# Encoder stages one slot later, their statistics split over two slots, and the last output sum on VectorE

## The chip, the cores and the metric

The kernel runs on one core of a Trainium2 chip. A core has five engines with queues of their own: TensorE (PE: matmuls and transposes, with weight loads shown as PEld), VectorE (DVE), ScalarE (ACT), GpSimd (POOL) and SyncE (SP, which issues the DMAs here). PE writes into PSUM, of which the kernel uses eight banks of 128 x 512 fp32. The metric is the device time of one execution in microseconds.

## The reference

One encoder layer over a context of 77 tokens, and one decoder layer over 2048 tokens, for 2 batches, width 512, 16 heads of 32, feed-forward width 2048, all in fp32 and with norms ahead of each part:

```python
x = x + _mha(_ln(x, enc_n1_s, enc_n1_b), _ln(x, ...), enc_in_w, ..., enc_out_w, ..., eb)   # src: 77 tokens
h = _ln(x, enc_n2_s, enc_n2_b)
memory = x + (jax.nn.relu(h @ enc_ff1_w.T + enc_ff1_b) @ enc_ff2_w.T + enc_ff2_b)
yn = _ln(y, dec_n1_s, dec_n1_b)                                                            # tgt: 2048 tokens
y = y + _mha(yn, yn, dec_sa_in_w, ..., sb)              # causal, with a relative bias
y = y + _mha(_ln(y, dec_n2_s, dec_n2_b), memory, dec_ca_in_w, ..., cb)
h = _ln(y, dec_n3_s, dec_n3_b)
y = y + (jax.nn.relu(h @ dec_ff1_w.T + dec_ff1_b) @ dec_ff2_w.T + dec_ff2_b)
```

`_mha` projects to q, k and v, takes softmax(q k / sqrt(32) + bias) v by heads, and projects out.

## The kernel before

The order of all work is written out by hand, each engine executing its instructions in the order of the program, and waits between engines by semaphores.

The first part is the decoder's causal self-attention. Its 2048 tokens of a batch are four blocks of 512. A *unit* is one tile of 128 query tokens (t) of one group of four heads (g) in one block (b, m): 16 units a block, 128 in all. For a unit, PE computes the scores of the four heads in pieces of up to four key tiles, one bank for each head (line L374); VectorE reads the banks into `pp` and takes the maximum, by L383 for the far keys and L390 for the last two tiles, where the bias is added; ScalarE takes the exp (L404); PE transposes the probabilities (`turn`, L424); ScalarE and VectorE copy the transposes to `pts` (L430, L428); PE multiplies them with v (`values`, L452). Scores run two units ahead of values. The banks come from a ring (`bank()` gives the one that was taken longest ago; `values` takes one out while its sum is held).

Between a unit's turn and the next scores, a *slot* runs side work: first the list `light[n]`, then the projections `jobs[n]` of coming blocks (q_job L215, part_job L1038, out_job L251), then the list `late[n]`. A list `behind[n]` runs after scores of a later unit and before the values. The slots hold, among others, the norm of coming blocks (`norm_load`, `norm_stats`, `norm_center`, `norm_turn`, the last with a bank for each token tile that ScalarE, L310, or VectorE, L312, empties) and the whole encoder.

The encoder is a generator of 28 stages, numbered from 0 here. Both batches' 77 tokens stand in `e`, a stretch of `pp` that the small units of the first two blocks leave free; its weights of 1 MB each are loaded into stretches of `vv` that are still free, two stages ahead of use.

| stage | work |
|---|---|
| 0 to 9 | first norm, q, k, v, scores and softmax |
| 10 | turn_p(0): transposes of batch 0's probabilities (L632), copied by VectorE (L633) |
| 11 | times_v(0) (L640), turn_p(1) |
| 12 | rows_of batch 0 (output projection, L593; sum by VectorE, L596), times_v(1) |
| 13 | rows_of batch 1; load of a bias row |
| 14 | `stats`: for each batch bn_stats (L557), bn_aggr, an add (L560) on VectorE and a power on POOL (L561) |
| 15 | centring on VectorE (L567), add of the bias row on POOL (L651) |
| 16 | turned: transposes (L573), scale and shift to `nTa` by VectorE (L579) |
| 17 to 20 | first(i): L585, relu on VectorE (L647), and the load of a later weight |
| 21 | turned again, without scale (copies L577) |
| 22 to 25 | second(i): L756, sums on VectorE (L759), a load |
| 26, 27 | the cross-attention's keys and values (L585, L593), stored to DRAM (L773, L774) |

Before, stages 0 to 9 are in `late[0]` to `late[9]`, 10 to 12 in `late[11]` to `late[13]`, 13 in `light[14]`, 14 in `behind[15]`, and 15 to 27 in `late[16]` to `late[28]`. Slots 0 to 15 belong to the block m = 0, 16 to 31 to m = 1; unit 32 begins m = 2, whose probabilities need the stretch of `pp` in which the encoder works.

The second part of the kernel runs the feed-forward of all eight blocks with cross-attention beside it. The products are of the Strassen-Winograd kind: seven block products and sums instead of eight products. `second_product` finishes each with four sums on VectorE (L1554 to L1561) into `mixed` and one 128 x 512 sum on POOL into `ys` (L1564); `store` then issues the output DMAs (L1570). The last block's last product ends the kernel.

Of the kernel before, what the change touches and what calls it, by code (L numbers as in the profile page):

```python
# [12 lines left out]
ALU = mybir.AluOpType  # L13
# [5 lines left out]
B, T, S, D = 2, 2048, 77, 512  # L19
# [35 lines left out]
def tile_encoder_decoder(ctx: ExitStack, tc: tile.TileContext, ins, out):  # L55
    nc = tc.nc
    x, src = ins["x"], ins["ctx_1024"]
# [3 lines left out]
    def wchunk(name, c0, n=D):  # L61

        return ins[name][:, c0 : c0 + n].rearrange("(c p) o -> p c o", p=P)
# [18 lines left out]
    def row_into(t, name):  # L82
        i = _ROWS.index(name)
        nc.sync.dma_start(t, ins["rows"][i : i + 1, :].to_broadcast([P, D]))
# [74 lines left out]
    with (  # L159
# [20 lines left out]
        def bank():  # L180

            ring.append(ring.pop(0))
            return psum[:, ring[-1], :]
# [168 lines left out]
        def exps(k):  # L352

            for _ in range(min(k, len(late_exps))):
                late_exps.pop(0)[1]()
# [152 lines left out]
        def encoder():  # L508
# [28 lines left out]
            def weight(i, view):  # L537

                w = vv[:, 4 * i : 4 * i + 4, :]
                nc.sync.dma_start(w, view)  # L540
                return w

            def load_row(name):
                i = _ROWS.index(name)
                nc.sync.dma_start(row, ins["rows"][i : i + 1, :].to_broadcast([S, D]))
# [4 lines left out]
            ws = {}  # L550
            keep = {}

            def stats():
                for b in range(B):
                    st = sm.tile([P, 6], F32, name="bnst", tag="bnst")
                    mv = sm.tile([P, 2], F32, name="emv", tag="emv", bufs=2)
                    nc.vector.bn_stats(st[:S], e[:, b, :])  # L557
                    nc.vector.bn_aggr(mv[:S], st[:S])
                    rs = sm.tile([P, 2], F32, name="ers", tag="ers", bufs=2)
                    nc.vector.tensor_scalar_add(rs[:S, 0:1], mv[:S, 1:2], EPS)  # L560
                    nc.gpsimd.tensor_tensor(rs[:S, 1:2], rs[:S, 0:1], mhalf[:S, 0:1], ALU.pow)  # L561
                    keep["norm", b] = mv, rs
# [27 lines left out]
            def rows_of(xT, f0, b, w, add, dst):  # L590
                mm = bank()
                for c in range(NC):
                    nc.tensor.matmul(  # L593
                        mm[:S, :], xT[:, f0 + c, ts(b, S)], w[:, c, :], start=(c == 0), stop=(c == NC - 1)
                    )
                nc.vector.tensor_tensor(dst, mm[:S, :], add, ALU.add)  # L596
# [59 lines left out]
            def stage():  # L656
                stats()
                ws["q"] = weight(1, wchunk("enc_in_wT", 0))
                ws["k"] = weight(2, wchunk("enc_in_wT", D))
                ws["v"] = weight(3, wchunk("enc_in_wT", 2 * D))  # L660
                load_row("enc_bv")
# [56 lines left out]
            yield stage  # L718

            def stage():  # L720
                rows_of(oTa, 0, 1, ws["o"], e[:, 1, :], e[:, 1, :])
                load_row("enc_ff2_b")

            yield stage
            yield stats

            def stage():
                for b in range(B):
# [224 lines left out]
        gp, ve = nc.gpsimd, nc.vector  # L953
# [126 lines left out]
        blocks = [(b, m) for b in range(B) for m in range(NMB)]  # L1080
        NU = NC * TB
        jobs = {n: [] for n in range(-1, len(units) + NU)}
        light = {n: [] for n in range(-1, len(units) + NU)}
        late, behind = {n: [] for n in light}, {n: [] for n in light}

        for x, (b, m) in enumerate(blocks):
            u = x * NU
# [27 lines left out]
            for t in range(TB):  # L1115
                end = x == len(blocks) - 1
# [68 lines left out]
                norm_turn(0, 0, t - 2, apart=True)  # L1185
                warm(6)
        for n, stage in enumerate(encoder()):
            if n == 13:
                light[n + 1].append(stage)
            elif stage.__name__ == "stats":  # L1190
                behind[n + (n >= 10)].append(stage)
            else:
                late[n + (n >= 10)].append(stage)
        light[-1].append(lambda: row_into(bo, "dec_sa_out_b"))
        light[0].append(lambda: [self_bias(relg, vg, g) for g in range(1, NC)])
        light[1].append(lambda: make_bias(0, rel, v))
# [38 lines left out]
        def y_of(x, t):  # L1235
            return ys[x % 3][:, t, :]
# [113 lines left out]
        for n, k in enumerate((0, 2, 4, 10)):  # L1350
# [17 lines left out]
        TWO = (  # L1368
            ("11", "11", 0, True, "11"),
            ("S1", "T1", 1, True, "22"),  # L1370
            ("S2", "T2", 0, False, "12"),
            ("S4", "22", 1, False, "12"),
            ("S3", "T3", 0, False, "22"),
            ("12", "21", 1, True, "11"),
            ("22", "T4", 0, False, "21"),
        )
# [53 lines left out]
        def next_w(c):  # L1430
            used[0] += 1
            assert used[0] <= fed[0]
            return w_ring[(used[0] - 1) % len(w_ring)].rearrange("p (c o) -> p c o", c=c)
# [14 lines left out]
        mixed = oflat[:, H * S : H * S + 12 * P].rearrange("p (k n) -> p k n", n=P)  # L1448
# [51 lines left out]
        def start_turn():  # L1500
            p = turn_of[0] % 2
            turn_of[0] += 1
            return pairs[p], pairs[1 - p]
# [32 lines left out]
        def second_product(x, j, part):  # L1536
            if j == 0 and part == 0:
                chains[0] = start_turn()
            name, by, chain, fresh, to = TWO[j]
            i1, i2 = chains[0][chain]  # L1540
            for k in range(2 * part, min(2 * part + 2, 7)):
                bank_i, col = ((i1, 0), (i1, 1), (i1, 2), (i2, 1), (i2, 2), (i2, 0), (i2, 3))[k]
                lhs, w = lefts[j][k], next_w(4)
                for c in range(4):
                    nc.tensor.matmul(  # L1545
                        psum[:, bank_i, ts(col, P)], lhs[:, c, :], w[:, c, :],
                        start=fresh and k in (0, 3) and c == 0, stop=c == 3, skip_group_check=True,
                    )
            one = psum[:, i1, :].rearrange("p (k n) -> p k n", n=P)
            two = psum[:, i2, :].rearrange("p (k n) -> p k n", n=P)  # L1550
            c0 = 4 * (j % 2)
            if part == 1:
                nc.scalar.copy(mixed[:, 11], one[:, 0])
                ve.tensor_tensor(  # L1554
                    mixed[:, c0 : 9 : 8 - c0], one[:, 1:3], mixed[:, 11:12].to_broadcast([P, 2, P]), ALU.add
                )
            if part < 3:
                return
            ve.tensor_tensor(mixed[:, 9:11], two[:, 1:3], mixed[:, 8:9].to_broadcast([P, 2, P]), ALU.add)
            ve.tensor_tensor(mixed[:, c0 + 1 : c0 + 4 : 2], two[:, 0:2], mixed[:, 9:11], ALU.add)  # L1560
            ve.tensor_tensor(mixed[:, c0 + 2], two[:, 3], mixed[:, 10], ALU.add)  # L1561
            r, c = int(to[0]) - 1, int(to[1]) - 1
            dst = ys[x % 3][:, 2 * r : 2 * r + 2, ts(c, TOK)]
            gp.tensor_tensor(dst, dst, mixed[:, c0 : c0 + 4].rearrange("p (t o) n -> p t (o n)", t=2), ALU.add)  # L1564
            done = [t for t in ((0, 1) if j == 5 else (2, 3) if j == 6 else ())]
            b, m = blocks[x]

            def store():
                for t in done:
                    nc.sync.dma_start(out_rows[b, m, :, t, :], y_of(x, t))  # L1570

            if x == len(blocks) - 1:
                store()
            elif done:
                after[x * per + FIRST + 4 * j + 3 + 3] = store
# [152 lines left out]
        end = len(units)  # L1728
# [13 lines left out]
        def score_next():  # L1742
            n, k0, kn = stream[at[0]]
            scores(n, k0, kn)
            scored_to[n] = k0 + kn
            at[0] += 1
# [5 lines left out]
        while i < len(stream):  # L1752
            n = stream[i][0]
            pair = [p for p in stream[i : i + 2] if p[0] == n]
            while scored_to.get(n) != size[n]:
                score_next()
            while any(u == n for u, _ in late_exps):
                exps(1)
            ends = pair[-1][1] + pair[-1][2] == size[n]
            turn(pair)  # L1760
            if n == end - 2:
                for _, k0, _ in pair:
                    feed(k0 + 4)
            turned_to[n] = pair[-1][1] + pair[-1][2]
            if ends and n + 1 < end:
                slot(n + 1)
            exps((0, 2, 1, 1)[units[n][1]])
            for _ in range(2 if len(pair) > 1 and units[n][1] else 1):
                if may_score():
                    score_next()  # L1770
            if ends:
                for f in behind[n + 1]:
                    f()
            values(pair)
            while may_score() and (len(pair) > 1 or units[n][1] == 0):
                score_next()
            i += len(pair)
# [68 lines left out]
```

## Time and profile before

| | us |
|---|---|
| median of 3 runs | 2768.12 (2767.57 to 2771.48) |
| profiled execution, whole time | 2771.65 |
| its span, first to last instruction | 2769.9 |
| PE busy | 2724.6 |
| DVE, ACT, POOL busy | 1807.0, 1538.8, 915.6 |
| mean granted PE clock | 0.995 of full speed |

The span is 1.75 us shorter than the profiled execution's time, and that is 3.5 us over the median. A row of the timeline gives start and length in us, engine, line, operation, output and inputs, and the count of merged instructions; in brackets stands the idle time ahead of it and the instruction that ended that. A row of the windows gives busy us (and instructions) of PE, PEld, DVE, ACT and POOL, then the granted PE clock, the DMA share and GB/s.

### The profile page before, as it was taken

The numbers are of one execution on the slowest core, as the hardware profiler recorded it, in microseconds if no ns is written. First come the engines' busy times: TensorE is split into PE (matmuls) and PEld (weight loads), VectorE is DVE, ScalarE is ACT, GpSimd is POOL, SyncE is SP. The second block draws the span as 40 slices with busy tenths as digits, with TensorE's granted clock in tenths as the row PEclk, the third lists the DMA queues.
The fourth block names the chain that finished last, engine by engine and source line by source line (L and its number), as shares of the span: only waits on it lengthen the run. The fifth ranks groups of instructions, "written<-read, shape, count | busy, mean of one in ns | idle before, by whom it ended". The sixth has DMA issues, their size and how long they took to land.

```text
span 2769.9 us, 67113 instructions
## 1 busy us (share of the span) xinstructions
PE 2724.6 (98%) x26294; PEld 2154.4 (78%) x26294; DVE 1807.0 (65%) x5312; ACT 1538.8 (56%) x2993; POOL 915.6 (33%) x777
## 2 busy tenths in 40 slices
PE   9999999999999999999999999999999999999998
PEld 5577776677776567676677777898989898989898
DVE  5775587787776587677687783556464646464645
ACT  3444567667777557677667786444444444444431
POOL 1501135300100413213200003364646464646456
PEclk9999999999999999999999999999999999999999
DMA  8433345311112422233211004565657564656465
GB/s 225 141 97 113 106 124 178 118 55 48 47 40 70 130 78 68 72 100 115 95 50 35 29 29 158 184 227 160 225 160 239 170 223 162 222 162 222 148 225 183
DMA packets 282254, 362.47 MB, mean 131 GB/s; under 512 B 39072, under 2 KB 156624, under 8 KB 281810
## 3 DMA queue, kind: packets, MB, share of 16 engines
q1 hardware_dynamic: 281938, 358.18, 41.4%
q8 instruction: 208, 3.41, 0.5%
q14 instruction: 108, 0.88, 0.1%
HBM read 314.49 MB, written 43.59 MB: 129 GB/s over the span
## 4 chain that ended last, share of the span: by engine, by line
PE 89%; DVE 4%; ACT 3%; issue 1%; POOL 1%; DMA 1%; SPq 0%; POOLq 0%; DVEq 0%; ACTq 0%
PE psum L424 17%; PE psum L1516 14%; PE psum L1545 12%; PE psum L374 9%; PE psum L452 8%; PE psum L1038 4%; PE psum L251 4%; PE psum L215 4%; PE psum L1676 3%; PE psum L1633 3%; ACT pp L404 3%; DVE pp L383 2%; PE psum L860 2%; PE psum L830 1%; PE psum L868 1%
## 5 line engine op out<-in xcount | busy, mean ns | idle before, releaser
L404 ACT ACTIVATE pp<-pp,nm 128x128 f32<-128x128 f32 (+15 forms) x512 | 611.8, 1201 | 34.5 <-DVE nm L399 34.0
L383 DVE TENSOR_SCALAR_CACHE_REDUCE pp<-psum 128x512 f32<-128x512 f32 (+3 forms) x1024 | 555.5, 591 | 75.0 <-PE psum L374 73.4
L424 PE MATMUL psum<-ident,pp 128*128 128x128 f32 x4352 | 536.4, 278 | 20.2 <-ACT pp L404 13.5
L430 ACT COPY pts<-psum 128x512 f32<-128x512 f32 (+2 forms) x736 | 386.5, 580 | 298.9 <-PE psum L424 258.0
L424 PEld LDWEIGHTS psum<-ident,pp 128*128 128x128 f32 x4352 | 478.5, 142 | 79.4 <-issue 24.9
L374 PE MATMUL psum<-kT,q 32*128 32x512 f32 (+3 forms) x2560 | 321.6, 559 | 4.6 <-ACT nT L310 2.6
L452 PEld LDWEIGHTS psum<-pts,vv 128*32 128x32 f32 x8704 | 226.7, 110 | 122.5 <-DVE pp L383 67.5
L428 DVE COPY pts<-psum 128x512 f32<-128x512 f32 (+3 forms) x400 | 249.5, 654 | 106.6 <-PE psum L424 104.4
L1545 PE MATMUL psum<-pp 128*128 128x128 f32 x2560 | 304.5, 276 | 1.9 <-POOL pp L956 1.6
L1545 PEld LDWEIGHTS psum<-pp 128*128 128x128 f32 x2560 | 296.3, 192 | 8.6 <-issue 2.8
L452 PE MATMUL psum<-pts,vv 128*32 128x128 f32 x8704 | 279.5, 276 | 6.7 <-DVE pp L383 4.2
L956 POOL TENSOR_TENSOR pp<-pp 128x512 f32<-128x512 f32 x159 | 212.6, 1354 | 126.5 <-DMA pp<-in_dec_ff_wT_dram 66.5
L1516 PE MATMUL psum<-vv,pp 128*128 128x256 f32 x1024 | 236.2, 381 | 0.0
L374 PEld LDWEIGHTS psum<-kT,q 32*128 32x128 f32 x2560 | 138.4, 183 | 125.6 <-issue 53.6
L1516 PEld LDWEIGHTS psum<-vv,pp 128*128 128x128 f32 x1024 | 190.3, 190 | 25.8 <-issue 0.5
L390 DVE CUSTOM_DVE_ANT_0 pp<-psum,bias 128x256 f32<-128x256 f32 (+1 forms) x512 | 196.2, 411 | 13.8 <-PE psum L374 13.6
L1529 DVE TENSOR_TENSOR kT<-kT,psum 128x512 f32<-128x512 f32 x96 | 65.8, 686 | 191.1 <-PE psum L1516 190.9
L1516 PE MATMUL psum<-nT,pp 128*128 128x256 f32 x768 | 174.1, 380 | 0.0
L1532 ACT ACTIVATE kT<-kT,vecs 128x256 f32<-128x256 f32 x192 | 87.0, 501 | 156.6 <-DVE kT L1529 155.9
L489 POOL TENSOR_TENSOR oT<-rirows,oT 128x512 f32<-128x512 f32 x30 | 38.4, 1280 | 377.9 <-DMA rirows<-rec 269.8
L1516 PEld LDWEIGHTS psum<-nT,pp 128*128 128x128 f32 x768 | 144.2, 190 | 20.3 <-issue 1.6
L266 POOL TENSOR_TENSOR xr<-xr,row_dec_sa_out_b 128x512 f32<-128x512 f32 x30 | 38.2, 1274 | 352.9 <-DMA xr<-in_x_dram 304.9
(243 smaller groups left out, 3907.5 us busy)
## 6 DMA issues: line engine op xcount, KB each, us to landing
pp<-w_d SPq DMA_DIRECT2D x520, 256.0 KB
pp<-in_dec_ff_wT_dram SPq DMA_DIRECT2D x112, 256.0 KB
wqk<-in_dec_sa_in_wT_dram SPq DMA_DIRECT2D x76, 256.0 KB
bias<-tzg SPq DMA_DIRECT2D x128, 128.0 KB
pp<-wo_d SPq DMA_DIRECT2D x56, 256.0 KB
vv<-in_enc_ff_wT_dram SPq DMA_DIRECT2D x8, 1024.0 KB
xr<-in_x_dram SPq DMA_DIRECT2D x32, 256.0 KB
vv<-y SPq DMA_DIRECT2D x32, 256.0 KB
```

Source lines behind the costliest of these rows:

```text
L215: nc.tensor.matmul(mm, w[:, c, :], nTs[b, m][:, c, :], start=(c == 0), stop=(c == NC - 1))
L374: nc.tensor.matmul(banks[r][:, : kn * P], q[rows4(r), ts(t, P)], kT[rows4(r), g, k0 * P : (k0 + kn) * P], start=True, stop=True,)
L383: nc.vector.tensor_scalar(p[:, k0 : k0 + far], s[:, :far], 1.0, None, ALU.mult, ALU.max, accum_out=st["mx"][:, r, c : c + 1],)
L390: nc.vector.tensor_tensor_reduce(p[:, k0 + far : i + 1], s[:, far:kn], near[:, 2 - (kn - far) :], 1.0, LOWEST, ALU.add, ALU.max, accum_out ...
L404: nc.scalar.activation(p, p, AF.Exp, bias=nm, accum_out=to)
L424: nc.tensor.transpose(pt[:, ts(x, P)], state[n]["p"][r][:, k], ident)
L428: nc.vector.tensor_copy(pts[:, : len(load), :], pt[:, :w])
L430: nc.scalar.copy(pts[:, : len(load), :], pt[:, :w])
L452: nc.tensor.matmul(ot[rows4(r)], vv[:, k, ts(g * HC + r, HD)], got.pop((n, k, r)), start=k == k0 and (whole or not begun), stop=k == k1 - ...
L956: engine.tensor_tensor(out, a, b, ALU.subtract)
L1516: nc.tensor.matmul(mm[:, ts(f, TOK)], a[:, c, ts(f, P)], b[:, c, :], start=fresh and f == 0 and c == 0, stop=c == 1, skip_group_check=True,)
L1545: nc.tensor.matmul(psum[:, bank_i, ts(col, P)], lhs[:, c, :], w[:, c, :], start=fresh and k in (0, 3) and c == 0, stop=c == 3, skip_group_ ...
```

## The change

The stages 10 to 12 go from `late[11]`–`late[13]` to `late[12]`–`late[14]`. Stage 13 goes from `light[14]` to `light[15]` and begins with the statistics of batch 0; stage 14, now the statistics of batch 1 alone, goes from `behind[15]` to `light[16]`, ahead of that slot's projections. The stages 15 to 27 go from `late[16]`–`late[28]` to `late[17]`–`late[29]`. The list `behind` is gone. In `second_product` the sum into `ys` of the last block's last product runs on VectorE; all others stay on POOL.

```diff
-            def stats():
-                for b in range(B):
+            def stats(batches=range(B)):
+                for b in batches:
...
             def stage():
+                stats([0])
                 rows_of(oTa, 0, 1, ws["o"], e[:, 1, :], e[:, 1, :])
                 load_row("enc_ff2_b")
 
             yield stage
-            yield stats
+            yield lambda: stats([1])
...
-        late, behind = {n: [] for n in light}, {n: [] for n in light}
+        late = {n: [] for n in light}
...
         for n, stage in enumerate(encoder()):
-            if n == 13:
-                light[n + 1].append(stage)
-            elif stage.__name__ == "stats":
-                behind[n + (n >= 10)].append(stage)
+            if n in (13, 14):
+                light[n + 2].append(stage)
             else:
-                late[n + (n >= 10)].append(stage)
+                late[n + 2 * (n >= 10)].append(stage)
...
-            gp.tensor_tensor(dst, dst, mixed[:, c0 : c0 + 4].rearrange("p (t o) n -> p t (o n)", t=2), ALU.add)
+            end = x == len(blocks) - 1 and j == len(TWO) - 1
+            (ve if end else gp).tensor_tensor(
+                dst, dst, mixed[:, c0 : c0 + 4].rearrange("p (t o) n -> p t (o n)", t=2), ALU.add
+            )
...
-            if ends:
-                for f in behind[n + 1]:
-                    f()
             values(pair)
```

## The prediction

> **What bounds the kernel now.** I read the page first, then the waits of TensorE (PE) between 96 and 350 us, which is where the moved encoder stages lie, then the timeline of those slots, and last the last fifteen microseconds.
>
> ```profile
> span 2769.9 us, 67113 instructions
> PE 2724.6 (98%) x26294; PEld 2154.4 (78%) x26294; DVE 1807.0 (65%) x5312; ACT 1538.8 (56%) x2993; POOL 915.6 (33%) x777
> PE 89%; DVE 4%; ACT 3%; issue 1%; POOL 1%; DMA 1%; SPq 0%; POOLq 0%; DVEq 0%; ACTq 0%
> ...
> PE psum L424 <- DVE mx L390: 2.7, 2, 2.0
> PE psum L374 <- ACT nT L310: 2.1, 1, 2.1
> PE psum L424 <- ACT nT L310: 1.4, 1, 1.4
> ```
>
> PE is busy for 98% and makes 89% of the chain, so a change that only reorders work can win no more than the idle time of PE, 2769.9 - 2724.6 = 45 us in the whole span, and the time in which PE runs slowly. The change touches slots 11 to 29 and the tail. In the wait rows (total, times, longest) two stalls lie inside the moved stretch: 2.1 us before scores L374, and 2.0 of the 2.7 us before transposes L424. The 1.4 us stall comes before slot 11 ends; nothing ahead of it moves, so it stays.
>
> **Part 1: slot 11, the bank of a transposed norm.** Columns: start, length, engine, line, operation, count.
>
> ```profile
> 110.01 1.27 PE L632 MATMUL psum<-ident,pp 77*77 77x77 f32 x16
> 111.20 0.48 PE L374 MATMUL psum<-kT,q 32*128 32x128 f32 x2
> ...
> 112.26 1.48 ACT L310 ACTIVATE nT<-psum,vecs 128x128 f32<-128x128 f32 x4
> ...
> 113.79 0.81 PE L374 MATMUL psum<-kT,q 32*128 32x128 f32 x6 [2.10 <-ACT nT L310]
> ...
> 114.53 1.51 PE L452 MATMUL psum<-pts,vv 128*32 128x128 f32 x24
> ...
> 115.97 3.68 PE L424 MATMUL psum<-ident,pp 128*128 128x128 f32 x16
> ```
>
> Eight banks go round in a ring; one is held by the sums, seven are left. Slot 11 takes two for the norm's tokens 2 and 3, then turn_p(0) (L632) takes four, then the four heads' scores: the second head meets the bank of token 2, which ScalarE empties only at 112.26 + 1.48 = 113.74, behind the exps. With turn_p(0) one slot later the scores take the four banks before it and run at once. So do the values (L452 x24); of the transposes the first load gets a free bank and the second meets token 2's bank. PE then does two short things in place of L632: 8 scores (about 0.5) and 24 value products. The same shapes elsewhere give the price:
>
> ```profile
> 51.46 0.86 PE L452 MATMUL psum<-pts,vv 128*32 128x128 f32 x24
> 52.25 1.97 PE L424 MATMUL psum<-ident,pp 128*128 128x128 f32 x16
> ```
>
> 110.1 + 0.5 + 0.86 + a quarter of 1.97 gives idle from about 111.95 instead of 111.7, still until 113.79: **0.3 us** less. ScalarE sets that end and isn't changed. That is little; the second half of the price is the clock. The x24 above took 1.51 instead of 0.86 and the x16 3.68 instead of 1.97. The windows' view says why (length, PE, PEld, DVE, ACT, POOL, granted clock):
>
> ```profile
> 106.22:109.64 3.42, 2.02 (x17) 1.78 (x18) 3.38 (x19) 2.78 (x9) 0.86 (x1) 1.00 0.00 0
> 109.64:113.05 3.41, 2.05 (x23) 1.78 (x21) 3.15 (x10) 3.41 (x11) 0.00 (x0) 1.00 0.03 7
> 113.05:116.46 3.41, 2.67 (x33) 1.99 (x34) 1.15 (x10) 0.69 (x2) 3.26 (x3) 0.50 0.01 2
> 116.46:119.88 3.42, 3.42 (x16) 3.31 (x16) 0.89 (x2) 1.64 (x5) 1.74 (x2) 0.50 0.00 0
> ...
> 157.42:160.84 3.42, 2.61 (x14) 2.40 (x15) 3.19 (x14) 1.43 (x3) 0.54 (x1) 1.00 0.02 5
> ...
> 1133.65:1137.06 3.41, 3.16 (x28) 1.11 (x28) 3.41 (x15) 3.41 (x7) 2.01 (x2) 1.00 0.00 0
> 1137.06:1140.47 3.41, 3.41 (x46) 3.03 (x37) 1.69 (x11) 1.20 (x4) 3.33 (x4) 0.50 0.00 0
> ```
>
> I laid the windows on one grid of 3.41 us, and every half-clock spell of this trace fills whole cells of it: two cells, 6.8 us, behind this stall. A cell with 2.02 us of PE work keeps the clock and one with 2.05 loses it, and so does one with 3.16, which is nearly all 32-row scores (L374). So it is not busy time alone; narrow work seems to count little (my reading, from three rows). The cell 109.64 to 113.05 held 77-row transposes and two 32-row scores; after the change it holds 0.9 us of full-row value products and a first load of 128-row transposes, and idles 1.1 instead of 1.4 us. I expect it to keep the clock. Price of the spell: (1.51 - 0.86) + (3.68 - 1.97) + half of the 0.81 of the six scores, about **2.8 us**; bounds 0 (the spell stays) and 2.8.
>
> The row gives half clock behind a cell that was 60% busy. [...]
>
> **Part 2: the statistics, slot 15 to 16.**
>
> ```profile
> 154.75 1.53 PE L424 MATMUL psum<-ident,pp 128*128 128x128 f32 x12
> 155.41 0.69 DVE L557 BATCH_NORM_STATS2 bnst<-pp 77x6 f32<-77x512 f32 x1
> ...
> 157.34 0.15 DVE L560 TENSOR_SCALAR ers<-emv 77x1 f32<-77x1 f32 x1
> 157.65 0.42 DVE L390 CUSTOM_DVE_ANT_0 pp<-psum,bias 128x256 f32<-128x256 f32 x1 [0.16 <-issue]
> ...
> 158.23 0.63 PE L424 MATMUL psum<-ident,pp 128*128 128x128 f32 x4 [1.95 <-DVE mx L390]
> ```
>
> VectorE does both batches' statistics between the two pieces of unit 16's score readings; the readings of the second piece (L390) start at 157.65 and not at 155.5, and the fourth load of unit 15's transposes waits 1.95 us for the bank. Without the 155.41 to 157.6 block L390 ends about 2.15 earlier, at about 156.0, before PE needs it (154.75 + 1.53 = 156.28). The ring positions of scores and transposes stand to each other as before. **1.95 us** won. The block is split in two of 1.05 us. Batch 0's stands in slot 15 ahead of the output rows, whose products then come with k5 and k3 behind: VectorE waits for PE there. Batch 1's stands in slot 16 ahead of v1 and v6; v6's add waits for ScalarE's copy of v1, which waits for exps. I cost both at nothing; without cover 1.05 each, so 0 to 2.1, and I take 0. POOL's two powers follow each; nothing on POOL is due before the centring. Queued behind the statistics on VectorE are the adds of k5/k3 and v6 only.
>
> **Part 3: centring and turning, slots 16 to 18.**
>
> ```profile
> 162.24 1.14 PE L374 MATMUL psum<-kT,q 32*128 32x512 f32 x8
> ...
> 163.87 0.99 DVE L567 TENSOR_SCALAR pp<-pp,emv,ers 77x512 f32<-77x512 f32 x2
> ...
> 166.15 2.74 PE L424 MATMUL psum<-ident,pp 128*128 128x128 f32 x20
> ...
> 174.54 2.29 PE L374 MATMUL psum<-kT,q 32*128 32x512 f32 x14
> 174.72 2.22 DVE L579 TENSOR_SCALAR pp<-psum,vecs 128x77 f32<-128x77 f32 x8
> ...
> 177.83 1.30 PE L452 MATMUL psum<-pts,vv 128*32 128x128 f32 x40
> ...
> 235.94 1.79 PE L374 MATMUL psum<-kT,q 32*128 32x512 f32 x16
> 237.85 1.30 PE L452 MATMUL psum<-pts,vv 128*32 128x128 f32 x40
> ```
>
> Undisturbed, a 7-tile unit goes from scores to values in 237.85 - 235.94 = 1.91 us. In slot 17, with eight L579 on VectorE ahead of the score readings, it takes 177.83 - 174.54 = 3.29: 1.4 us lost. In slot 16 scores, values and second scores should hand over after about 2.7 us, and take 166.15 - 162.24 = 3.9, from the centring and from exps that part 2's stall delayed: 1.2 us lost, and some 0.3 in the transposes. After: slot 16 has no centring and its exps come 2 us earlier: about 0.1 lost. Slot 17 has the centring, 0.99 instead of 2.22 of VectorE, without the transposes that covered 0.6: 1.4 - 1.15 + 0.6, some 0.75. Slot 18 has the turning, behind one product q1: 1.4 again (8 tiles instead of 7; 1.2 to 2.9 if nothing covers it). Sum: 2.9 - 2.25 = **0.65 us** won.
>
> **Part 4: what else moves.** In slots 13 and 14 turn_p(1), its four copies and times_v sit behind k6 and k7 instead of with q0 and k1; I count -0.2 for a bank that comes late (-1.4 to 0). The feed-forward stages 17 to 27 each go a slot on with their 1 MB weight loads in the SP queue, and so do the small row loads of stages 13 and 16; each load keeps two slots of lead, and the loads queued behind it (biases, q and k tiles) are for slots later. I take nothing. The last one, the stores of the cross keys and values, must end before unit 32's scores overwrite that stretch of pp:
>
> ```profile
> 326.41 7.03 PE L593 MATMUL psum<-vv,pp 128*77 128x512 f32 x16
> ...
> 334.19 0.30 SPq L774 DMA_DIRECT2D cv_d<-pp  x1
> ...
> 342.95 1.79 PE L374 MATMUL psum<-kT,q 32*128 32x512 f32 x16
> ...
> 363.33 1.79 PE L374 MATMUL psum<-kT,q 32*128 32x512 f32 x16
> ```
>
> The store follows the rows' products (7.03 long) by 0.8 us and leaves 363.33 - 334.19 = 29 us. A slot later the rows start where slot 29's products end, at 342.95, and the store goes out near 351: 12 us are left. Nothing lost.
>
> **Part 5: the tail.**
>
> ```profile
> 2754.53 0.69 DVE L956 TENSOR_TENSOR pp<-kT 128x512 f32<-128x512 f32 x1
> 2764.76 1.26 POOL L1564 TENSOR_TENSOR vv<-vv,oT 128x512 f32<-128x512 f32 x1 [4.99 <-DVE oT L1561]
> ```
>
> Nothing runs beside this sum, and the last stores wait for it. VectorE does a sum of that shape in 0.69 (beside a busy POOL it takes longer, but POOL is idle here): 1.26 - 0.69, and about 0.08 for the hand-over between engines: **0.65 us**, all on the path.
>
> **Sum.** Waits 0.3 + 1.95 + 0.65 - 0.2 + 0.65 = 3.35; with the spell 2.8, 6.15 us. The profiled execution took 2771.65 (span 2769.9 and 1.75 around it), 3.5 above the median of 2768.12; I take the difference off the median: **2762.0 us**.
>
> **Rivals.** (1) Waits only: the half-clock spell comes anyway, since 1.84 us of idle stay in slot 11, or the runs of the median hadn't it: 2768.12 - 3.35 = 2764.8. For it: 2.02 and 2.05 us busy are a thin line. (2) One spell more goes: the 1.95 us stall lay across an edge of the grid here (157.42) and kept its clock; in other runs it can fall into one cell and cost half of 3.41. 6.15 + 1.7: 2760.3. (3) The delays only move: slots 17 and 18 lose all that slot 16 gains and what part 2 frees comes back at slot 13 or 14 (1.4): gain about 1, 2767.1. Against it: the order of the banks in the ring, counted through slot 12 to 18. (4) Slower: in slot 18 the turning keeps the score readings back for its full 2.2 + 0.7 us, unit 19 being the largest of the block: 1.5 more than counted, and the idle, once above some 1.4 us in a cell of narrow score products, halves the clock for two cells, 3.4 us. With the spell at slot 11 kept: 3.35 - 1.5 - 3.4 = -1.55, 2769.7; a second such cell at slot 13 makes it 2773. Against it: the same block in slot 17 lost 1.4 and kept the clock.
>
> **Chances.** Forecast 0.55, rival 1 0.20, rival 2 0.10, rival 3 0.08, rival 4 0.07. A measurement of this kernel tells about 0.2%, 5.5 us, from no change. Of the forecast's case four in five lie beyond that, with rival 2 that is 0.54 faster; rivals 1 and 3 and the rest 0.41; slower 0.05. Range 2758.3 (rival 2 and 2 us for spells elsewhere, as the whole later work shifts on the grid) to 2767.0 (rival 3).
>
> **What would show it.** Right: no stall over 0.3 us before the transposes at 156 us; the first at slot 11 about 1.8 us, before L424 instead of L374, and clock 1.00 behind it; in slot 18 scores to values some 3.3 us; last sum on VectorE, 0.69. Wrong: a new wait over 1 us in slots 12 to 15 or 18, or half clock near 115 us.

## The result and the profile after

The changed kernel took 2764.27 us in the median of 20 runs (lowest 2762.87), the kernel before 2768.51 beside it (20 runs, 2766.60 to 2772.53). The ratio is 0.9982, 95% interval 0.9975 to 0.9989: 5.0 us faster by the ratio (3.0 to 6.9), 4.2 by the medians. Two executions of the changed kernel, at 2833.87 and 5527.29 us, stand far from all others, and the ratio leaves them out. The gain is 0.18%, a little less than the 0.2% that the prediction held for the least a measurement can tell, but the interval excludes no change; 2762.0 was forecast. The profiled execution took 2766.41 us.

From the page of the changed kernel, its engines:

```profile
span 2764.6 us, 67114 instructions
PE 2721.8 (98%) x26294; PEld 2151.6 (78%) x26294; DVE 1807.3 (65%) x5313; ACT 1538.8 (56%) x2993; POOL 915.2 (33%) x776
```

PE has the same 26294 instructions; one instruction has gone from POOL's count and one has come to VectorE's. The span fell by 5.3, PE's busy time by 2.8 with the same instructions, so that the clock has to be looked at, and its idle time by 2.5. The waits of PE between 96 and 350 us, changed kernel (total, times, longest):

```profile
PE psum L424 <- ACT nT L310: 3.2, 2, 1.8
PE psum L452 <- DVE pp L383: 2.0, 6, 0.6
PE psum L424 <- DVE mx L390: 0.7, 1, 0.7
```

The 2.0 us stall that the statistics made is gone from the row of L390; 0.7 is the other one, which was there before. The 2.1 us stall before scores L374 has become one of 1.8 before transposes L424, beside the 1.4 of an earlier slot. The row of the values grew from 1.6 to 2.0. Now the timeline of slots 11 and 15 to 18, PE with VectorE's rows that matter:

```profile
110.28 0.50 PE L374 MATMUL psum<-kT,q 32*128 32x128 f32 x8
110.72 0.86 PE L452 MATMUL psum<-pts,vv 128*32 128x128 f32 x24
113.98 1.97 PE L424 MATMUL psum<-ident,pp 128*128 128x128 f32 x12 [1.81 <-ACT nT L310]
115.74 4.89 PE L215 MATMUL psum<-nT,wqk 128*128 128x512 f32 x8
...
153.28 1.97 PE L424 MATMUL psum<-ident,pp 128*128 128x128 f32 x16
...
157.03 0.65 DVE L557 BATCH_NORM_STATS2 bnst<-pp 77x6 f32<-77x512 f32 x1
...
158.63 1.14 PE L374 MATMUL psum<-kT,q 32*128 32x512 f32 x8
161.43 2.74 PE L424 MATMUL psum<-ident,pp 128*128 128x128 f32 x20
...
169.29 1.79 PE L374 MATMUL psum<-kT,q 32*128 32x512 f32 x16
171.65 1.30 PE L452 MATMUL psum<-pts,vv 128*32 128x128 f32 x40 [0.58 <-DVE pp L383]
...
179.87 3.63 PE L374 MATMUL psum<-kT,q 32*128 32x512 f32 x16
180.12 2.21 DVE L579 TENSOR_SCALAR pp<-psum,vecs 128x77 f32<-128x77 f32 x8
183.43 1.52 PE L452 MATMUL psum<-pts,vv 128*32 128x128 f32 x48
```

At 153.28 the transposes are one group of sixteen with no idle time in it. Slot 16 goes from scores to transposes in 161.43 - 158.63 = 2.80 us (3.91 before), slot 17 from scores to values in 2.36 (3.29 before), slot 18 in 3.56. But the x12 at 113.98 takes 1.97 where twelve of 1.97 / 16 each would take 1.5, and L215 4.89 where it takes 3.60 in a trace below: a half-clock cell is still there (granted clock 0.50 from 114.91 to 118.33 us).

One number compares profiles closely: the *stretch* from the eight scores of unit 11 (start near 104) to the first eight products of slot 30 (near 345). It holds all of the moved stages and the same PE work in every kernel here, but for e4's filling. A *cell* is, as in the prediction, one length of 3.41 us on the grid that the half-clock spells of a trace fill: in the changed kernel they start at 114.91, 517.69, 1343.71 and 1678.22 us, the last three 118, 360 and 458 times 3.413 us behind the first, and last 3.41 or 6.83 us; a fifth, at 2763.66, is cut by the end. The ends of the stretch are, in the changed kernel:

```profile
104.25 1.55 PE L374 MATMUL psum<-kT,q 32*128 32x512 f32 x8
345.09 1.99 PE L1039 MATMUL psum<-nT,wqk 128*128 128x256 f32 x8
```

| kernel | stretch, us | half-clock cells (3.41 us) in it |
|---|---|---|
| before (348.92 - 104.07) | 244.85 | 2 |
| e3 (before, but for the tail; 345.31 - 103.31) | 242.00 | 0 |
| after | 240.84 | 1 |
| e5 (after once more; 343.38 - 104.21) | 239.17 | 0 |
| e4 (after, stall filled) | 239.14 | 0 |
| e2 (shift alone) | 242.28 | 1 |
| e1 (statistics alone) | 241.17 | 0 |
| e9 (split, no shift) | 241.33 | 1 |
| e6, e12 (token tile 2 on VectorE) | 237.53, 237.52 | 0 |
| e7, e8 (turning shared chunk by chunk; e8 with token tile 2) | 239.69, 238.04 | 0 |
| e10, e11 (turning shared by batch) | 236.46, 236.50 | 0 |

The one kernel that was traced twice without a half-clock cell gave 237.53 and 237.52 (e6, e12), and e4, which differs from e5 by its filling alone, lies 0.03 from it. So one cell cost 240.84 - 239.17 = 1.67 in these profiles, two cost 244.85 - 242.00 = 2.85, and the waits alone won 242.00 - 239.17 = 2.83.

### The profile page after: what moved, and what is told of

Read it like the earlier page. It is cut to its first block, busy times and chain, and to the rows that moved or that the text cites. A ratio compares the mean times of both kernels' runs of the same rounds, so it can differ in the third digit from the quotient of the medians.

```text
span 2764.6 us, 67114 instructions
## 1 busy us (share of the span) xinstructions
PE 2721.8 (98%) x26294; PEld 2151.6 (78%) x26294; DVE 1807.3 (65%) x5313; ACT 1538.8 (56%) x2993; POOL 915.2 (33%) x776
## 3 DMA queue, kind: packets, MB, share of 16 engines
q8 instruction: 208, 3.41, 0.5%
## 4 chain that ended last, share of the span: by engine, by line
PE 91%; DVE 4%; ACT 3%; issue 1%; POOL 1%; DMA 0%; SPq 0%; ACTq 0%; DVEq 0%; POOLq 0%
PE psum L424 18%; PE psum L1515 14%; PE psum L1544 12%; PE psum L374 9%; PE psum L452 8%; PE psum L1039 5%; PE psum L215 4%; PE psum L251 4%; PE psum L1678 3%; PE psum L1635 3%; ACT pp L404 3%; DVE pp L383 2%; PE psum L861 2%; PE psum L831 1%; PE psum L869 1%; PE psum L585 1%
## 5 line engine op out<-in xcount | busy, mean ns | idle before, releaser
L424 PE MATMUL psum<-ident,pp 128*128 128x128 f32 x4352 | 535.8, 278 | 19.7 <-ACT pp L404 13.3
L424 PEld LDWEIGHTS psum<-ident,pp 128*128 128x128 f32 x4352 | 477.5, 142 | 78.8 <-DVE pp L383 23.8
L374 PE MATMUL psum<-kT,q 32*128 32x512 f32 (+3 forms) x2560 | 320.0, 559 | 1.8 <-ACT kT L231 0.7
L374 PEld LDWEIGHTS psum<-kT,q 32*128 32x128 f32 x2560 | 137.5, 183 | 122.1 <-issue 53.1
L390 DVE CUSTOM_DVE_ANT_0 pp<-psum,bias 128x256 f32<-128x256 f32 (+1 forms) x512 | 196.1, 411 | 12.4 <-PE psum L374 12.4
```

The lines of the kernel that those rows point to most:

```text
L374: nc.tensor.matmul(banks[r][:, : kn * P], q[rows4(r), ts(t, P)], kT[rows4(r), g, k0 * P : (k0 + kn) * P], start=True, stop=True,)
L390: nc.vector.tensor_tensor_reduce(p[:, k0 + far : i + 1], s[:, far:kn], near[:, 2 - (kn - far) :], 1.0, LOWEST, ALU.add, ALU.max, accum_out ...
L424: nc.tensor.transpose(pt[:, ts(x, P)], state[n]["p"][r][:, k], ident)
```

## The experiments

All twelve were timed against the kernel before on the same chip. The first four took the change apart; theory: waits for banks and the half-clock cells make the gain; rivals: the shift alone, or the place of the statistics alone, makes all of it.

**e1: the statistics ahead of the projections, nothing else moved.**

```diff
             elif stage.__name__ == "stats":
-                behind[n + (n >= 10)].append(stage)
+                light[n + 1].append(stage)
```

> The kernel before, with one edit: both batches' statistics in the light list of slot 15 (ahead of k5 and k3) instead of behind the scores of unit 16. All other stages where they were. Theory (the statistics' stall and what follows it are most of the gain): no wait over 0.3 us before the transposes near 156 us, slot 16 hands over from scores to transposes in about 2.8 to 3.0 instead of 3.9 us, so some 2.9 us less (1.95 + 0.9); the 2.1 us stall of slot 11 and the half clock behind it stay. Rival (the shift of the stages is what pays): under 0.7 us.

2767.78 us beside 2769.18, ratio 0.9992 (0.9983 to 1.0001). In the stretch it won 242.00 - 241.17 = 0.83 against e3, which has no half-clock cell either. The timeline of e1:

```profile
150.98 2.12 PE L374 MATMUL psum<-kT,q 32*128 32x256 f32 x8
153.03 1.97 PE L424 MATMUL psum<-ident,pp 128*128 128x128 f32 x16
```

A miss. The stall before the transposes is gone, but the second scores take 2.12 us, where e9 does the same eight in 0.71: VectorE does 2.1 us of statistics for both batches and then the adds of the projections, and reads the first scores only at 151.79, 2.5 us behind their start (0.9 in e9). The statistics are not free wherever they stand ahead of the projections.

**e2: every stage from 10 on one slot later, the statistics still behind the scores and in one piece.**

```diff
             if n == 13:
-                light[n + 1].append(stage)
+                light[n + 2].append(stage)
             elif stage.__name__ == "stats":
-                behind[n + (n >= 10)].append(stage)
+                behind[n + 2].append(stage)
             else:
-                late[n + (n >= 10)].append(stage)
+                late[n + 2 * (n >= 10)].append(stage)
```

> The kernel before, with the stages 10 to 27 one slot later, but the statistics of both batches still behind the scores, now of unit 17 (behind slot 16), and the last sum on POOL. Theory (the shift alone gives only slot 11): the stall of slot 11 0.3 us shorter and up to 1.7 us from one half-clock cell, while the statistics' block of 2.1 us now delays the score readings of unit 17 and costs 1 to 2 us there: 0 to 1.5 us less in all. Rival (the shift is what pays): 3 us less or more.

2766.47, ratio 0.9988 (0.9979 to 0.9997). The stretch is 242.28 with one cell, so about 242.28 - 1.67 = 240.6 without: some 1.4 won by the shift, and 240.6 - 239.15, again 1.4 or so, by the place of the statistics. The stall moved to the next unit:

```profile
164.13 0.66 PE L424 MATMUL psum<-ident,pp 128*128 128x128 f32 x4 [1.24 <-DVE mx L390]
```

Neither half makes the gain alone.

**e3: the tail alone.** The diff is the one of `second_product` in the change; nothing else.

> The kernel before, with only the very last output sum on VectorE. Theory: the sum takes 0.69 instead of 1.26 us and starts about 0.06 earlier, the end comes 0.65 us sooner; too little for the median to show, the trace shows it. Rival (hand-over or stores set the end): under 0.2 us between the sum's predecessor and the end of the span.

2769.19, ratio 1.0002 (0.9993 to 1.0010): nothing that a median could show. The trace does. VectorE's last small sum before, then two rows of e3, then the last two sums of the changed kernel:

```profile
2764.40 0.28 DVE L1561 TENSOR_TENSOR oT<-psum,oT 128x128 f32<-128x128 f32 x1
```

```profile
2760.04 0.28 DVE L1561 TENSOR_TENSOR oT<-psum,oT 128x128 f32<-128x128 f32 x1
2760.36 0.69 DVE L1565 TENSOR_TENSOR vv<-vv,oT 128x512 f32<-128x512 f32 x1
```

```profile
2759.79 0.28 DVE L1560 TENSOR_TENSOR oT<-psum,oT 128x128 f32<-128x128 f32 x1
2760.10 0.69 DVE L1564 TENSOR_TENSOR vv<-vv,oT 128x512 f32<-128x512 f32 x1
```

From the start of VectorE's last small sum to the end of the span it is 5.50 us before, 4.86 in e3 and 4.81 after: 0.64 and 0.69 won (the spans are given to 0.1 us). What e3 showed beside that was not looked for. Up to the tail it is the code of before, and its stall in slot 11 is as long (2.10), yet nothing runs at half clock behind it:

```profile
113.02 0.50 PE L374 MATMUL psum<-kT,q 32*128 32x128 f32 x6 [2.10 <-ACT nT L310]
113.45 0.86 PE L452 MATMUL psum<-pts,vv 128*32 128x128 f32 x24
114.24 1.97 PE L424 MATMUL psum<-ident,pp 128*128 128x128 f32 x16
```

The cells that the prediction priced at 2.8 us are thus not a property of the program.

**e4: the changed kernel with ten idle transposes in slot 11's stall**, into a bank that is free there.

```diff
+        def fill(k):
+            for _ in range(k):
+                nc.tensor.transpose(psum[:, ring[0], :P], ident, ident)
+
+        late[11].append(lambda: fill(10))
```

> The changed kernel, with ten more 128x128 transposes of the identity into the oldest bank at the end of slot 11, whose result nobody reads: PE works some 1.1 us where it stood idle, the path is the same. Theory (the idle time in one 3.41 us cell of the clock grid sets the half clock): idle of slot 11 falls from 1.8 to about 0.7 us at the same time of resumption, no half clock near 115 us, so about 1.7 us less than the changed kernel in an execution which had one such cell there. Rival (the clock falls for another reason, or the added work costs its own time): the half clock stays, or the time grows by up to 1.1 us.

2764.74, ratio 0.9981 (0.9972 to 0.9990), no faster than the changed kernel. The timeline of e4:

```profile
109.13 1.25 PE L1218 MATMUL psum<-ident 128*128 128x128 f32 x10
112.92 1.53 PE L424 MATMUL psum<-ident,pp 128*128 128x128 f32 x12 [0.72 <-ACT nT L310]
```

PE resumes 112.92 - 103.20 = 9.72 us behind the start of the stretch, the changed kernel 113.98 - 104.25 = 9.73: the end of the wait is set by ScalarE, with the filling and without it. Full clock behind it proves nothing, since the next run has that without filling.

**e5: the changed kernel once more**, in the second group of runs, to see whether its half-clock cell comes again. No edit.

> The changed kernel once more, beside the three that follow. Theory: 3 to 6 us under the kernel before; in the profile the stretch from the scores of unit 11 to the first product of slot 30 takes 239.1 us without a half-clock cell, 1.7 more for each cell that falls into it (240.8 with one, as in its first profile).

2765.11 beside 2770.74, ratio 0.9979 (0.9970 to 0.9988). The same stall of 1.83 us, and full clock:

```profile
113.96 1.53 PE L424 MATMUL psum<-ident,pp 128*128 128x128 f32 x12 [1.83 <-ACT nT L310]
115.33 3.60 PE L215 MATMUL psum<-nT,wqk 128*128 128x512 f32 x8
```

The windows, laid on the grid that the half-clock spells of each trace give (e5's first begins at 515.4 us, which is 118 cells of 3.413 behind 112.65), show what differs. Columns as in the prediction; the changed kernel, then e5, then e3:

```profile
111.50:114.91 3.41, 1.60 (x17) 1.35 (x14) 1.50 (x11) 2.90 (x9) 1.52 (x2) 1.00 0.02 5
114.91:118.33 3.42, 3.42 (x10) 1.87 (x9) 1.51 (x4) 2.13 (x9) 3.42 (x3) 0.50 0.00 0
```

```profile
109.24:112.65 3.41, 2.90 (x46) 2.17 (x44) 3.09 (x15) 3.41 (x10) 0.00 (x0) 1.00 0.04 10
112.65:116.06 3.41, 2.10 (x14) 1.75 (x15) 1.33 (x3) 2.65 (x9) 2.69 (x3) 1.00 0.00 0
```

```profile
108.54:111.95 3.41, 2.38 (x26) 2.11 (x24) 3.14 (x10) 3.41 (x11) 0.00 (x0) 1.00 0.03 7
111.95:115.36 3.41, 2.34 (x40) 2.02 (x41) 1.49 (x11) 1.44 (x4) 2.93 (x3) 1.00 0.01 2
```

In the changed kernel's profile the whole stall lies in one cell, PE is busy 1.60 of 3.41 us there, and the next cell runs at half clock. In e5 and e3 an edge of the grid cuts the stall in two, neither cell has less than 2.10 us of PE work, and the clock stays. Four more traces with this stall agree: in e2 (cell from 110.41) and e9 (from 111.68) it lies whole in one cell and the next runs at half clock; in e1 (edge at 112.13) and e7 (at 111.90) an edge cuts it and the clock stays. The trace of before is the exception: the edge at 113.05 cuts its stall, and the clock falls nevertheless; why stays open. Where the grid lies differs from one execution to the next: the changed kernel has an edge at 114.91 us in its first trace, and at 112.65 and 116.06 in e5. Half clock followed this stall of 2 us in four of the eight traces that have it (before, the changed kernel, e2, e9), and not in the others (e1, e3, e5, e7).

The busy time of a cell does not decide alone. A cell of e3 and one of e9:

```profile
152.91:156.33 3.42, 1.72 (x10) 1.62 (x11) 3.15 (x14) 0.91 (x2) 1.10 (x2) 1.00 0.02 5
```

```profile
930.86:934.28 3.42, 1.59 (x7) 1.07 (x8) 1.96 (x6) 2.62 (x12) 3.26 (x3) 1.00 0.22 77
```

Behind both the clock is 1.00 too, though e3's cell holds 1.7 of the 1.96 us that the statistics make PE wait; but cells with 2.01 us in e5 (from 1338.02) and 2.44 in e10 (from 1335.64) are followed by half clock. Those two hold over 1 us of 32-row scores, the two above hold none. That fits the prediction's reading that narrow work counts little, but it does not explain the changed kernel's 1.60 us, lost without any such scores, and no run tried it by itself. What in a cell decides stays open.

**e6: the norm's token tile 2 emptied by VectorE**, in the changed kernel. If ScalarE's late emptying sets the 1.8 us stall, this ends it.

```diff
-                    on = nc.vector if x == 1 and t % 2 else nc.scalar
+                    on = nc.vector if x == 1 and t else nc.scalar
```

> The changed kernel, with the norm's token tile 2 of block 1 emptied from its bank by VectorE (as tile 3 already is) instead of ScalarE, where it stood behind four exps. Theory (ScalarE's order holds the bank in slot 11): the bank is free near 111.8 instead of 113.8, the wait of 1.8 us falls under 0.8, no half-clock cell there, the stretch takes about 238 us: 1 us under the changed kernel without a cell, 2.8 under it with one. Rival (VectorE is as late, since tile 3 and the scores' readings queue behind it): the wait stays over 1.3 us, now for VectorE.

2762.19, ratio 0.9970 (0.9958 to 0.9981); e5, on the same chip, had 2765.11. The timeline of e6:

```profile
109.84 2.63 DVE L312 TENSOR_SCALAR nT<-psum,vecs 128x128 f32<-128x128 f32 x8
112.62 1.06 PE L424 MATMUL psum<-ident,pp 128*128 128x128 f32 x8 [0.20 <-DVE nT L312]
```

The wait fell from 1.8 to 0.2, the stretch by 239.17 - 237.53 = 1.64. **e12**, the same kernel in the third group, gave 2762.98 beside 2769.63, ratio 0.9974 (0.9965 to 0.9984), and a stretch of 237.52.

> The changed kernel with token tile 2 on VectorE, once more. Theory: ratio near 0.997 again, the stretch 237.5 us without a half-clock cell.

**e7: the turning of slot 18 shared between VectorE and ScalarE, chunk by chunk**, in the changed kernel, to take the 1.64 us that slot 18 loses. **e8** is e7 and e6 together.

```diff
+                    elif n == "n2" and c % 2:
+                        nc.scalar.activation(
+                            d, s, AF.Identity, bias=vec(f"enc_{n}_b", c), scale=vec(f"enc_{n}_s", c)
+                        )
```

> The changed kernel, with every second of the eight scale-and-shift steps of the encoder's second turning (slot 18) on ScalarE instead of VectorE. Theory (the turning's block on VectorE ahead of unit 19's score readings costs 1.6 us): scores to values of unit 19 fall from 3.56 to some 2.5 us, 1.0 us less in all. Rival (ScalarE's exps of unit 18 are still running, so its half comes late and unit 19 waits for banks instead): no gain, 3.5 us or more.

> The changed kernel with both: token tile 2 on VectorE and the turning shared. Theory: the gains add, the stretch takes about 237 us without a half-clock cell, median 2 to 3 us under the changed kernel's in the same rounds. Rival: one of them takes back the other's gain, under 1 us.

e7 2766.49, ratio 0.9982 (0.9973 to 0.9991); e8 2765.96, 0.9981 (0.9972 to 0.9990). A miss in both; the timeline of e7:

```profile
177.33 4.21 PE L374 MATMUL psum<-kT,q 32*128 32x512 f32 x16
...
177.96 0.42 ACT L579 ACTIVATE pp<-psum,vecs 128x77 f32<-128x77 f32 x1 [2.38 <-DVE pp L583]
178.41 0.62 DVE L583 TENSOR_SCALAR pp<-psum,vecs 128x77 f32<-128x77 f32 x2 [0.49 <-ACT pp L579]
178.80 0.73 ACT L579 ACTIVATE pp<-psum,vecs 128x77 f32<-128x77 f32 x2 [0.43 <-DVE pp L583]
...
181.47 1.52 PE L452 MATMUL psum<-pts,vv 128*32 128x128 f32 x48
```

Scores to values grew from 3.56 to 181.47 - 177.33 = 4.14. The even and the odd chunks lie in one bank, and each engine starts only at a semaphore of the other, with 0.43 to 0.53 us of idle time at each turn: the work is shared but not done at the same time. The rows show this order, not who set it.

**e9: the split statistics without the shift of the other stages**, from the kernel before, to see whether the rows' products cover them, as the prediction has it.

```diff
                 stats([0])
                 rows_of(oTa, 0, 1, ws["o"], e[:, 1, :], e[:, 1, :])
...
-            yield stats
+            yield lambda: stats([1])
...
-            if n == 13:
-                light[n + 1].append(stage)
-            elif stage.__name__ == "stats":
-                behind[n + (n >= 10)].append(stage)
+            if n in (13, 14):
+                light[n + 2].append(stage)
```

> The kernel before, with stage 13 and the split statistics where the change puts them (batch 0 and the rows in slot 15, batch 1 in slot 16), all other stages unshifted and the last sum on POOL. It tells whether the output rows beside the statistics are what the statistics alone lacked. Theory (the rows' 3.5 us of products in slot 15 hide the statistics): no wait at the scores or transposes near 152 to 156 us, the stretch from unit 11's scores to slot 30 takes 239.5 to 240.2 us without a half-clock cell, 2 us under the kernel before (242.0) and over 1 us better than the statistics alone (241.2). Rival (the shift of the other stages is needed): 241 us or more.

2768.47, ratio 0.9996 (0.9987 to 1.0004). The timeline of e9:

```profile
153.64 0.71 PE L374 MATMUL psum<-kT,q 32*128 32x256 f32 x8
154.28 1.97 PE L424 MATMUL psum<-ident,pp 128*128 128x128 f32 x16
...
159.63 1.14 PE L374 MATMUL psum<-kT,q 32*128 32x512 f32 x8
...
163.35 2.74 PE L424 MATMUL psum<-ident,pp 128*128 128x128 f32 x20
```

No wait at 154, and scores of 0.71 where e1 has 2.12: split and with the rows' products behind the first of them, the statistics cost nothing here; which of the two does it was not tried apart. Slot 16, which here has the centring still, takes 163.35 - 159.63 = 3.72, nearly the 3.91 of before. The stretch is 241.33 with one cell, some 239.7 without, as expected. That the time stayed is not a contradiction: five half-clock spells lie in its profile, 23.9 us of half clock in all, as much as in that of before, and medians of these runs do not settle 1 or 2 us.

**e10: e6, and the turning shared by batch**, batch 1 by ScalarE from its own bank.

```diff
+                    elif n == "n2" and b:
+                        nc.scalar.activation(
+                            d, s, AF.Identity, bias=vec(f"enc_{n}_b", c), scale=vec(f"enc_{n}_s", c)
+                        )
```

> The changed kernel, token tile 2 on VectorE, and the second turning divided by batch: batch 0, with its own bank, by VectorE, batch 1 by ScalarE. Theory (two engines on one bank waited for each other in the earlier sharing; on a bank each they don't): VectorE's block is halved to 1.1 us, scores to values of unit 19 some 2.4 instead of 3.56 us, the stretch 236.4 us. Rival (ScalarE's part is late or the engines still take turns): 3.4 us or more, no gain over token tile 2 alone (237.5).

2762.57, ratio 0.9976 (0.9966 to 0.9986). The timeline of e10:

```profile
176.33 2.62 PE L374 MATMUL psum<-kT,q 32*128 32x512 f32 x16
176.44 1.33 ACT L579 ACTIVATE pp<-psum,vecs 128x77 f32<-128x77 f32 x4 [1.88 <-PE psum L573]
176.57 1.14 DVE L583 TENSOR_SCALAR pp<-psum,vecs 128x77 f32<-128x77 f32 x4
...
178.87 1.52 PE L452 MATMUL psum<-pts,vv 128*32 128x128 f32 x48
```

Now both engines run at the same time, four chunks each with no idle time between, and scores to values take 2.54. The stretch fell by 237.53 - 236.46 = 1.07. So it was VectorE's 2.21 us of turning, ahead of the score readings, that slot 18 lost.

**e11: e10, with the norm's odd token tiles first**, so that VectorE's emptying starts sooner.

```diff
-                    light[turned_at].append(lambda b=b, m=m, t=t, on=on: norm_turn(b, m, t, on=on))
+                    first_at = len(light[turned_at]) - 1
...
+                    turning = lambda b=b, m=m, t=t, on=on: norm_turn(b, m, t, on=on)
+                    light[turned_at].insert(first_at, turning) if x == 1 and t % 2 else light[turned_at].append(turning)
```

> As the one before, and in slots 10 and 11 the odd token tile of the norm is turned ahead of the even one, so that the bank which VectorE empties stands ahead in the ring of the one that ScalarE empties late. Theory: the wait of 1.43 us in slot 10 comes one load later in the transposes and falls by about 0.35 us; the stretch 236.0 us. Rival: VectorE is later with it or the norm's own input is, no change.

2762.60, ratio 0.9973 (0.9963 to 0.9982). The wait of slot 10 fell from 1.41 in e10 to 1.08, as expected, and a new one took it back in slot 11:

```profile
107.80 0.87 PE L423 MATMUL psum<-ident,pp 128*128 128x128 f32 x6 [1.08 <-ACT nT L309]
...
112.32 1.06 PE L423 MATMUL psum<-ident,pp 128*128 128x128 f32 x8 [0.53 <-ACT pts L429]
```

The stretch is e10's within 0.04. By the stretch, e6 with its repeat e12, e10 and e11 beat both kernels; by the times e6 does on one chip (2762.19, e5 2765.11, before 2770.74), with intervals of the ratio that still overlap e5's. Between these versions the runs do not decide.

## Why the prediction came out as it did

The direction, the range and the waits were right; the half-clock term was wrong in kind, and part of the agreement in the waits is luck. Point by point:

- **Part 1, the stall of slot 11 (0.3).** It came in the place and size foretold: 1.81 before L424 instead of 2.10 before L374, ended by ScalarE. From the start of the stretch to L215, without half-clock cells, it is 116.05 - 103.31 = 12.74 in e3 and 115.33 - 104.21 = 11.12 in e5; 1.20 of the difference is turn_p(0), which left the slot (L632 from 109.24 to L374 at 110.44 in e3). So 0.42 won.
- **Part 1, the clock (2.8, bounds 0 and 2.8).** The size was right for two cells, 2.85 by before and e3. The step that failed is that it was taken as gained whole: that before always has the cells, and that 1.8 us of stall would keep the clock. The expected busy time of the cell was of a grid that this execution did not have: the changed kernel's profile kept one cell at 1.67, so these two profiles differ by 1.2 and not 2.8, and e3 has none without the change. Half clock near 115 us was a sign of being wrong by the prediction's own list, and it came (from 114.91). The 2.8 was also read off an execution 3.5 us above the median and then taken off the median. What such cells brought on average is the rest: 4.2 by the medians less 3.5 of waits and tail (2.83 + 0.65) is 0.7, and the interval of the ratio leaves from about -0.5 to 3.4; the repeat, e5, gained 5.6 by the medians, which leaves 2.1. The size of this average stays open. The prediction named the waits alone as a rival, 2764.8, and gave it 0.20; the result, 2764.3, lies next to it.
- **Part 2, the statistics (1.95).** The mechanism was right: no idle time at 153.28. The size was a little more. From the first scores of slot 15 to the product behind its transposes it is 155.08 - 148.84 = 6.24 in e3 and 153.38 - 149.28 = 4.10 in e5, with the same PE work: 2.14 won. That their new places cost nothing was right too, and e1 and e9 show that this hangs on the split and the rows' products together, not on the place ahead of the projections alone.
- **Part 3, slots 16 to 18 (0.65).** Slot 16 won 3.91 - 2.80 = 1.11, where 1.1 of scores to transposes was counted; the 0.3 in its transposes did not come, the twenty still take 2.58 to the next product. Slot 17 lost 0.45 against 1.91 undisturbed, not 0.75. Slot 18 lost 3.56 - 1.92 = 1.64, not 1.4 (1.92 is a unit of its size undisturbed, 189.49 to 191.41 in the trace of before). Between these marks 1.11 + (1.38 - 0.45) - 1.64 = 0.40 was won. The transposes behind them change as well: those behind slot 18's values take 3.36 in e5 and 3.78 in e3. From the first scores of slot 16 to the end of those transposes, e3 takes 192.86 - 158.63 = 34.23, of which 4.29 is the product L585, and e5 186.38 - 156.93 = 29.45 without that product: 0.49 won in all. The mechanisms were right, the sizes off by 0.2 to 0.3 each, partly cancelling. (The prediction's 1.4 - 1.15 + 0.6 is 0.85 and not 0.75; its sum would be 0.55.)
- **Part 4 (-0.2).** No new wait came in slots 13 and 14: from the start of the stretch to the first scores of slot 15 it is 45.53 in e3 and 45.07 in e5, so slots 11 to 14 won 0.46, 0.42 of it in slot 11. The loss came where the prediction put nothing, with the stages 17 to 27. The turning without scale (stage 21) delays the readings of the next scores as that of slot 18 does, and moved from slot 22 to 23: from L251 in slot 22 to L305 behind slot 23 it is 264.63 - 238.29 = 26.34 in e3 and 258.52 - 231.80 = 26.72 in e5, with the same PE work, 0.38 lost. In slot 22 shorter transposes (3.35 for 3.78) made up for part of the delay, in slot 23 nothing did. The terms make 0.46 + 2.14 + 0.49 - 0.38 = 2.71 of the 2.83 measured; 0.12 is left. Nothing queued in SP or POOL shows among the waits. The last store went out at 340.02, 19.5 us before unit 32's scores at 359.50; the forecast 351 counted the 7 us of the rows' products twice.
- **Part 5 (0.65).** 0.64 in e3, 0.69 after, by spans given to 0.1 us. That VectorE takes longer beside a busy POOL shows in the trace of before: its 128 x 512 sums of L956 take 0.68 us in the seven cases where POOL stands still, and 0.63 to 1.80, in the median 1.10, in the 113 beside POOL's work. The last sum, with POOL idle, took 0.69 in both.

Waits of 2.7 in the stretch were forecast and 2.83 came, and with the tail 3.35 and about 3.5. That the sums lie so close is in part luck: slot 11 and the statistics brought 0.3 more than counted, slots 16 to 18 brought 0.2 less, and the loss of part 4 came from another stage. The rival of delays that only move and the slower one fell: slot 18 is the largest new loss, but no cell of half clock starts there in any profile. The rival of one more spell gone is not seen either: in e3 the stall of the statistics lay almost whole in one cell, and the clock stayed.

## What to carry to other kernels

Price a PE stall as its waits, worked out bank by bank, and the clock behind it as a chance, here four traces of eight, three of the four with the stall whole in one cell of the grid: compare two profiles of the same code before a half-clock spell is counted as the program's. Small changes are told apart by the time between two fixed instructions in traces of equal clock, which agreed within 0.01 us for the one kernel traced twice so, where medians of runs leave 1 to 2 us open. When a job is shared between two engines, share it by banks (scores to values took 4.14 us with one bank for both in e7, 2.54 with one each in e10), and when it is moved for cover, look whether its cover moves with it.

## What was not expected of the hardware

- The grid of 3.41 us lies differently in the two traces of the changed kernel (edges at 114.91 and 112.65 us), and the number of half-clock cells in the stretch differs with it (1 and 0). By the granted clock, the 33 runs of before in the first group have mean spans of 2770.3 us (0.995, 6 runs), 2767.5 (0.996, 19) and 2766.6 (0.997, 8).
- PE's busy time in a cell does not tell whether the next one keeps the clock: 1.59 (e9) and 1.72 us (e3) kept it, 1.60 (the changed kernel), 2.01 (e5) and 2.44 (e10) lost it. So the 2.02 kept and 2.05 lost of the prediction's windows are no edge. The cell with 3.16 us of mostly 32-row scores, which lost it before, recurs in e4, e9 and e11 (3.16 each, all lost); what weight such work has was not tried.
- VectorE and ScalarE taking turns at one bank in e7 paid 0.43 to 0.53 us at each turn, more than VectorE's time for one chunk (2.21 / 8 = 0.28).
